# Two cross-attention layers in fp32: a third buffer for the small weights, the last value products planned to the end, and a first input load cut by contraction chunks

## The chip, the cores and the metric

The kernel runs on one core of a Trainium2 chip. The metric is the device time of one launch in microseconds. Before the change three runs took 2079.56, 2083.08 and 2083.56 us, median 2083.08. TensorE is called PE here, VectorE DVE, ScalarE ACT, GpSimd POOL and SyncE SP; SP issues most loads, POOL most stores.

## The reference, cut to what matters

There are 8 batches of 100 query rows with 640 channels, a context of 722 rows with 1024 channels (77 text rows, 645 image rows), and 20 heads of 32 channels. Layer 1 takes the output of layer 0. All is fp32.

```python
def layer(x, ctx, l):                       # heads split and merged as usual
    text, ip = ctx[:, :77], ctx[:, 77:]
    q = x @ Wq
    k, v = text @ Wk, text @ Wv             # text keys and values
    ki, vi = ip @ Wk_ip, ip @ Wv_ip         # image keys and values
    text_out = softmax(q k^T * scale) v
    if l == 0:
        ip_out = softmax(q ki^T * scale) vi
    else:                                   # layer 1
        pt = softmax(q @ k^T * scale)       # over all channels, not per head
        sem = (pt @ text) @ ip^T * scale    # one map for all heads
        ip_out = (softmax(q ki^T * scale + 0.5 * sem) * mask) vi
    return (text_out + ip_out) @ Wo + bo + x
```

## The kernel before, in words

**Projections.** Keys and values of the context are by far the largest matmuls. `seven` forms them with seven products of half-size blocks where the plain way has eight; it needs sums of weight quarters (`weight_sums`, L127) and of context quarters (`token_sums`, L212). `token_sums` puts two adds on DVE (`s1`, then `s2`) and two on POOL (`s3`, and `s4`, which reads `s2`).

**First stage (L222 to L407).** A pool named "first" holds what only this stage needs. SP loads x of batches 0 and 1 (tile `xt`, L227), five chunks of the query weights (`wq0`, 128 rows of the contraction each, L230), the rest of x in three loads, the text, then the K and V weights. PE forms the queries of layer 0 (`psq`, L253): for each pair g of batches, five contraction chunks k, and in each five output chunks c. Their results go out by POOL's queue. Then, in an order written out by hand (L388), text keys and values of both layers follow (`text_k`, whose first products are `pskt`, then the seven products `pskt_a` to `pskt_e`; `text_v`). The sums of the text (`s_text`) have a tile of their own, formed as soon as the text is there.

**Main stage.** A unit u is a layer and a batch (16 of them); a chunk c is four heads. The list `ORDER` has 80 steps of one unit and chunk each. In the last ten the two last units are interleaved: steps 70 to 79 are (14,0), (14,2), (15,0), (15,2), (14,1), (14,3), (15,1), (15,3), (14,4), (15,4). In step n PE does, by hand-written order: scores of the first 512 keys (`sc`, L837), transposes 0 and 1 of the previous step's probabilities (`pspt`, L922), transposes 2 and 3, scores of the other 210 keys, transposes 4 and 5, and the values (`pv`, L944) of the previous step. Copies of transposes to SBUF (`pt`) are done by DVE (L929), for j = 2 and 5 by ACT (L927). ACT does the exponentials (L861) and half of the scaling (L889), DVE the maxima (L853) and sums.

**The planner.** Between these pieces PE gets projection products for later units. `production` (L957) makes a list of tasks, each group with a stretch of steps (a, b), and `spread` gives each task a time inside it. `between(n, a, b, small)` issues all tasks whose time lies below n + b, and with `apart` takes one more from the next 0.4 of a step if otherwise two small pieces would stand side by side. The last products of the last two units are `fifth_chunk`: keys (`psk`, L669) with some values, planned for steps 72.9 to 76.9, then values alone (`psv`, L675) from 76.9 to 78.6. Each such block of 128 context rows has its x tile loaded (`x<-ip_t`) and its values stored in DRAM and loaded again as `v`.

**Small work.** For each pair g of units, five `out_piece` (L746, products `pso`, DVE add at L757) form the layer's output, and for layer 0 five `q_piece` (L766) form the queries of layer 1. Each piece reads one tile of weights of 320 KB, `wo` (o or q), loaded by `load_wo` (L739) on SP in a ring of two buffers; there are 55 such loads. The output of the last pair is made by `last_out` (L798, products `pso_last`, L804) from weights that stay in SBUF; its last call for a unit also adds the residual on DVE (L811) and issues the store on SP (L812). After step 79 follow `last_out(0)`, six transposes of the last step, values, `last_out(1)`.

The order of PE is fixed by hand in the main stage; that of DVE, ACT, POOL and SP is made by the framework's scheduler when the kernel is built. Buffers of a pool are rings: a load or a write into a ring's tile waits until the readers of the tile that lay there before are done.

Of the kernel before, what the change touches and what calls it, by code (L numbers as in the profile page):

```python
# [9 lines left out]
F32 = mybir.dt.float32  # L10
# [4 lines left out]
P = 128  # L15
B = 8
S = 100
# [10 lines left out]
NC_ = C // P  # L28
# [6 lines left out]
HK = NCC // 2  # L35
# [3 lines left out]
PAIRS = [(2 * i, 2 * i + 1) for i in range(NU // 2)]  # L39
# [5 lines left out]
def two_layer_xattn(  # L45
# [17 lines left out]
    nc = tc.nc  # L63
# [3 lines left out]
    wpool = ctx.enter_context(tc.tile_pool(name="w", bufs=1))  # L67
# [144 lines left out]
    def token_sums(a11, a12, a21, a22, s1, s2, s3, s4):  # L212
        nc.vector.tensor_tensor(s1, a21, a22, ALU.add)
        nc.vector.tensor_tensor(s2, s1, a11, ALU.subtract)
        nc.gpsimd.tensor_tensor(s3, a11, a21, ALU.subtract)
        nc.gpsimd.tensor_tensor(s4, a12, s2, ALU.subtract)
        return {1: a11, 2: a12, 3: s4, 4: a22, 5: s1, 6: s2, 7: s3}


    TH = B * NT // 2  # L220
    TR = TH - 2 * P
    with ExitStack() as es:  # L222
        fp = es.enter_context(tc.tile_pool(name="first", bufs=1))
        pj.append(es.enter_context(tc.tile_pool(name="ps_first", bufs=6, space=PSUM)))
        xt = fp.tile([P, B, NC_, S], F32, tag="x", name="xt")
        wq0 = []
        nc.sync.dma_start(xt[:, :2], x_t[:, :2])  # L227
        for k in range(NC_):
            t = fp.tile([P, C], F32, tag="wr", name=f"wq0_{k}", bufs=NCC)
            nc.sync.dma_start(t, wq[0][k * P : (k + 1) * P, :])  # L230
            wq0.append(t)
        for g in range(1, B // 2):
            nc.sync.dma_start(xt[:, 2 * g : 2 * g + 2], x_t[:, 2 * g : 2 * g + 2])
        text = fp.tile([P, NCC, B * NT], F32, tag="text", name="text")
# [12 lines left out]
        for g in range(B // 2):  # L247
# [16 lines left out]
                )  # L264
            nc.gpsimd.dma_start(q_d[0][g], t)

        st = fp.tile([P, 4, HK, TH], F32, tag="s", name="s_text")
        sums = token_sums(
            *(text[:, HK * h : HK * (h + 1), TH * i : TH * (i + 1)] for i in range(2) for h in range(2)),
            *(st[:, i] for i in range(4)),  # L270
        )

        def text_k(l):
            t = fp.tile([P, 2, 512], F32, tag="ev", name=f"kt4_{l}", bufs=2)
# [110 lines left out]
        def sums_of(kind):  # L385
            weight_sums(kind, {"v": HC, "k": 2 * P}[kind], (nc.vector, nc.gpsimd))

        with tc.manual_schedule(engines={mybir.EngineType.PE}):  # L388
            sums_of("k")
            text_k(0)  # L390
            load_wk(wkt[1])
            text_v(0)
            sums_of("v")
            load_left(0)
            text_v_blocks(0)
            load_wv(wvt[1])
            sums_of("k")
            text_k(1)
            load_wk(wki[0])
            left_v(0)  # L400
            load_left(1)
            left_text()
            text_v(1)
            sums_of("v")
            text_v_blocks(1)
            sums_of("k")
            left_v(1)  # L407
# [180 lines left out]
    LAST = PAIRS[-1]  # L588
# [150 lines left out]

    def load_wo(kind, src, g):  # L740
        for c in range(NC_):
            t = wpool.tile([P, NC_, P], F32, tag="wo", name=f"{kind}_{g}_{c}", bufs=2)
            nc.sync.dma_start(t, src.rearrange("(k p) n -> p k n", p=P)[:, :, c * P : (c + 1) * P])
            wos[kind, g, c] = t

# [52 lines left out]
    def last_out(i, ks_):  # L798
        g = len(PAIRS) - 1
        if ks_[0] == 0:  # L800
            last_ps[i] = product_ps(f"pso_last_{i}")
        for k in ks_:
            for c in range(NC_):
                nc.tensor.matmul(  # L804
                    last_ps[i][:, c * S : (c + 1) * S], lhsT=last_w[c][:, k, :], rhs=hsg[g][:, i, k, :],
                    start=(k == 0 and c == 0), stop=(k == NC_ - 1), skip_group_check=True,
                )
        if ks_[-1] < NC_ - 1:
            return
        r = resg[g][:, i].rearrange("p c s -> p (c s)")  # L810
        nc.vector.tensor_tensor(r, last_ps[i][:, : NC_ * S], r, ALU.add)  # L811
        nc.sync.dma_start(out[LAST[i] % B], resg[g][:, i])  # L812
# [99 lines left out]

    pts = {}

    def transposes(u, c, j):
        if j == 0:
            emit(len(later))
            pts[u, c] = one.tile([P, 6, 4 * S], F32, tag="pt", name=f"pt_{u}_{c}")
        rows = P if j < 5 else NTAIL
        ps = ps_pt.tile([P, 512], F32, tag="pt", name=f"pspt_{u}_{c}_{j}")  # L920
        for i in range(4):
            nc.tensor.transpose(  # L922
                ps[:rows, i * S : (i + 1) * S], pr[u, c][:, i, j * P : j * P + rows], ident[:S, :S]
            )
        dst, src = pts[u, c][:rows, j, :], ps[:rows, : 4 * S]
        if j % 3 == 2:
            nc.scalar.copy(dst, src)  # L927
        else:
            nc.vector.tensor_copy(dst, src)  # L929
# [27 lines left out]
    def production():  # L957

        plan = []
        for i in range(1, len(PAIRS) - 1):  # L960
            tasks = pair_tasks(PAIRS[i])
            at = max(n for n, (t, _) in enumerate(tasks) if t == 2.15) + 1
            if i == B // 2 - 1:

                tasks = tasks[:at] + [(0.0, lambda: second_weights("v"))] + tasks[at:]
                tasks.append((0.0, lambda: second_weights("k")))
            elif i == len(PAIRS) - 2:
                tasks = tasks[:at] + [(0.0, last_weights)] + tasks[at:]
            plan.append((10 * (i - 1) - AHEAD, 10 * i - AHEAD, tasks))
        n = 5 * LAST[0]  # L970
        every = list(range(NB))
        by_chunks = [blocks_of(every, lambda j, xs, r=r: two_chunks(r, j, xs)) for r in range(2)]
        fifth = [
            blocks_of(every, lambda j, xs: fifth_chunk("kv" if j < 2 else "k", j, xs)),
            blocks_of(every[2:], lambda j, xs: fifth_chunk("v", j, xs)),
        ]
        plan.append((n - 10 - AHEAD, n + 2.9, by_chunks[0] + by_chunks[1]))
        plan.append((n + 2.9, n + 6.9, fifth[0]))
        plan.append((n + 6.9, n + 8.6, fifth[1]))
        return [task for a, b, tasks in plan for task in spread(a, b, tasks)]  # L980

    def spread(a, b, tasks):
# [91 lines left out]
    with tc.manual_schedule(engines={mybir.EngineType.PE}):  # L1074
        for _, f in pair_tasks(PAIRS[0]):
            f()
        load_q(0)
        load_vt(0)
        load_k(0, 0)
        todo = production()  # L1080
        done = [0]

        def next_task():
            todo[done[0]][2]()
            if todo[done[0]][0] and later:
                emit(1)
            done[0] += 1

        def make(until):
            while done[0] < len(todo) and todo[done[0]][1] < until:  # L1090
                next_task()

        mark = [0]

        def apart(until):

            while done[0] < len(todo) and todo[done[0]][1] < until and not any(
                t for t, _, _ in todo[mark[0] : done[0]]
            ):
                next_task()  # L1100
            mark[0] = done[0]

        def between(n, a, b, small):

            mark[0] = done[0]
            for i, (_, f) in enumerate(small):
                make(n + a + (b - a) * (i + 1) / (len(small) + 1))
                apart(n + b + 0.4)
                f()
            make(n + b)  # L1110
            apart(n + b + 0.4)

        make(0.0)
        last = None
        for n, (u, c) in enumerate(ORDER):
            at = small_work(n)
            loads(n)
            scores(u, c, 0)
            if n == len(ORDER) - 1:
                load_v(*last)  # L1120
                load_v(u, c)
            between(n, 0.0, 0.4, at[0])
            if last:
                transposes(*last, 0)
                transposes(*last, 1)
            between(n, 0.4, 0.6, at[1])
            if last:
                transposes(*last, 2)
                transposes(*last, 3)
            scores(u, c, 1)  # L1130
            if n == NC_ * LAST[0] - 1:
                load_q(LAST[1])
            between(n, 0.6, 0.8, at[2])
            if n < len(ORDER) - 2:
                load_v(u, c)
            if n + 1 < len(ORDER):
                load_k(*ORDER[n + 1])
            if last:
                transposes(*last, 4)
                transposes(*last, 5)  # L1140
            between(n, 0.8, 1.0, at[3])
            if last:
                values(*last)
            last = (u, c)
        last_out(0, [NC_ - 1])
        for j in range(6):
            transposes(*last, j)
        values(*last)
        last_out(1, [NC_ - 1])


# [44 lines left out]
```

## Time and profile before

| what | value |
|---|---|
| runs, us | 2079.56, 2083.08, 2083.56 |
| profiled execution, us | 2088.13 |
| its span, us | 2086.4 |
| PE busy | 2058.5 us, 99% |
| DVE, ACT, POOL busy | 988.3, 862.8, 379.8 us |
| SP's hardware queue | 184.48 MB, 32.6% of 16 engines' span |
| first matmul | 5.63 us |
| end of the last `psq` | 41.44 us |
| steps 76, 77, 78 (start to start of scores) | 11.02, 12.42, 10.29 us |
| last matmul ends, span ends | 2082.5, 2086.4 us |

The profile is of one execution, and times in it run from the span's start. Busy times of engines overlap, so the table does not add up to the span. A wait is written as "engine, tile, line, what released it: us in total, times, longest us". In a timeline, a row is a run of equal instructions with its start, its length, and in brackets the idle time ahead of it on that engine and what ended it. The granted clock is what the throttle of PE allowed, 1.00 being full speed.

### The profile page before, as it was taken

How to read it: one execution, taken by the hardware profiler on the slowest of the kernel's cores; microseconds unless marked ns; L12 is line 12 of the kernel's file. 1: busy time of each engine (PE TensorE's matmuls, PEld its weight loads, DVE VectorE, ACT ScalarE, POOL GpSimd, SP SyncE). 2: the span in 40 equal slices, each digit the busy share in tenths (PEclk: the TensorE clock that was granted, in tenths of full speed). 3: DMA queues.
4: the chain of work that ended last, by engine and by line, in shares of the span. 5: the costliest groups of instructions: out<-in, count | busy, mean ns of one | idle time of the engine just before them, and what ended most of it. 6: DMA issues, size and time to landing. Idle time of an engine off the chain costs nothing. (4 is left out here: it accounts for less than half of the span.)

```text
span 2086.4 us, 41767 instructions
## 1 busy us (share of the span) xinstructions
PE 2058.5 (99%) x16690; PEld 1641.6 (79%) x16690; DVE 988.3 (47%) x2526; ACT 862.8 (41%) x2830; POOL 379.8 (18%) x409
## 2 busy tenths in 40 slices
PE   8999999999999999999999999999999999999998
PEld 8676787777777777787788877887888778889786
DVE  2111221345554554444464554445455455667565
ACT  1001000245434544344444544445444445566576
POOL 3213211111110111111141111111111113223120
PEclk9999999999999999999999999999999999999999
DMA  9345232323333443352544443353344344545482
GB/s 350 108 134 165 87 87 78 113 75 96 103 99 119 119 118 88 96 162 81 157 121 131 124 117 81 103 156 94 85 112 132 104 122 136 158 119 142 126 227 73
DMA packets 299104, 255.58 MB, mean 123 GB/s; under 512 B 43102, under 2 KB 267794, under 8 KB 298910
## 3 DMA queue, kind: packets, MB, share of 16 engines
q1 hardware_dynamic: 279374, 184.48, 32.6%
q0 software_dynamic: 19536, 68.43, 9.8%
q8 instruction: 132, 2.16, 0.4%
q14 instruction: 62, 0.51, 0.1%
HBM read 183.93 MB, written 68.93 MB: 121 GB/s over the span
## 5 line engine op out<-in xcount | busy, mean ns | idle before, releaser
L861 ACT ACTIVATE p<-sc,st 100x512 f32<-100x512 f32 (+1 forms) x320 | 166.5, 528 | 227.3 <-DVE st L846 227.3
L929 DVE COPY pt<-pspt 128x400 f32<-128x400 f32 x320 | 175.9, 569 | 122.4 <-PE pspt L922 119.4
L861 ACT ACTIVATE p<-p,st 100x512 f32<-100x512 f32 (+1 forms) x320 | 177.0, 555 | 134.9 <-DVE st L853 134.5
L889 ACT ACTIVATE p<-p,st 100x512 f32<-100x512 f32 x320 | 209.6, 714 | 48.6 <-DVE st L883 48.2
L922 PE MATMUL pspt<-ident,p 100*128 100x100 f32 (+1 forms) x1920 | 212.2, 251 | 7.2 <-DVE res L757 2.5
L922 PEld LDWEIGHTS pspt<-ident,p 100*128 100x128 f32 (+1 forms) x1920 | 187.8, 138 | 37.2 <-issue 5.5
L528 PE MATMUL psv_a<-wv,x 128*128 128x397 f32 (+1 forms) x560 | 185.3, 473 | 2.0 <-ACT vo L174 2.0
L927 ACT COPY pt<-pspt 128x400 f32<-128x400 f32 (+1 forms) x160 | 77.9, 487 | 254.8 <-PE pspt L922 254.7
L528 PE MATMUL psv_d<-wv,s 128*128 128x320 f32 (+1 forms) x560 | 174.7, 454 | 0.0
L552 POOL DMA_DIRECT2D v_d<-vo x70 | 39.5, 564 | 723.6 <-DVE gst L520 386.4
L846 DVE TENSOR_REDUCE st<-sc 100x2 f32<-100x1024 f32 (+1 forms) x120 | 126.2, 1052 | 68.2 <-ACT p L861 37.8
L528 PEld LDWEIGHTS psv_a<-wv,x 128*128 128x128 f32 x560 | 103.1, 189 | 65.9 <-issue 9.4
L853 DVE CUSTOM_DVE_ANT_0 p<-sc,sem 100x512 f32<-100x512 f32 (+1 forms) x320 | 139.6, 490 | 25.4 <-PE sc L837 25.3
L528 PEld LDWEIGHTS psv_d<-wv,s 128*128 128x128 f32 x560 | 103.6, 190 | 56.0 <-issue 6.6
L536 PEld LDWEIGHTS psk_a<-x,wk 128*128 128x128 f32 x1120 | 132.3, 191 | 12.7 <-issue 9.4
L837 PE MATMUL sc<-k,q 32*100 32x210 f32 (+1 forms) x1280 | 140.6, 509 | 1.2 <-ACT p L861 0.6
L564 POOL DMA_DIRECT2D k_d<-ko x70 | 58.2, 831 | 448.6 <-DVE ko L200 426.6
L536 PE MATMUL psk_d<-s,wk 128*128 128x128 f32 (+1 forms) x1120 | 139.7, 277 | 0.0
L536 PE MATMUL psk_a<-x,wk 128*128 128x128 f32 (+1 forms) x1120 | 139.1, 277 | 0.0
L536 PEld LDWEIGHTS psk_d<-s,wk 128*128 128x128 f32 x1120 | 131.2, 191 | 8.2 <-issue 3.3
L503 PE MATMUL psk<-x,wk 128*128 128x256 f32 (+1 forms) x560 | 131.6, 383 | 0.0
L503 PEld LDWEIGHTS psk<-x,wk 128*128 128x128 f32 x560 | 102.1, 189 | 23.2 <-issue 7.9
(207 smaller groups left out, 3403.5 us busy)
## 6 DMA issues: line engine op xcount, KB each, us to landing
x<-ip_t SPq DMA_DIRECT2D x84, 512.0 KB
k<-k_d SPq DMA_DIRECT2D x80, 322.5 KB
v<-v_d SPq DMA_DIRECT2D x80, 320.0 KB
v_d<-vo POOLq DMA_DIRECT2D x70, 320.0 KB, 2.6
k_d<-ko POOLq DMA_DIRECT2D x56, 320.0 KB, 6.8
x<-ip_t SPq DMA_DIRECT2D x22, 532.0 KB
o<-wo SPq DMA_DIRECT2D x35, 320.0 KB
q<-wq SPq DMA_DIRECT2D x20, 320.0 KB
```

The source lines that it names most:

```text
L503: nc.tensor.matmul(ps[:, : 2 * n], lhsT=W["k", 4][:, k, :], rhs=xs[j][:, :, k, :n], start=(k == 0), stop=(k == NCC - 1),)
L528: nc.tensor.matmul(ps[:, :m], lhsT=sums[which][:, k, :P], rhs=w[:, k, :], start=(k == 0 and not go_on), stop=(k == HK - 1), skip_group_che ...
L536: nc.tensor.matmul(ps[:, r * n : (r + 1) * n], lhsT=W["k", WHICH[which]][:, k, r * P : (r + 1) * P], rhs=sums[which][:, k, :], start=(r == ...
L564: nc.gpsimd.dma_start(k_d[u][:, :, n0 : n0 + n], ko[0][:, h, :, :n])
L837: nc.tensor.matmul(sc[:S, i, : k1 - k0], lhsT=qs_[u][rows, c, :], rhs=ks[u, c][rows, k0:k1], start=True, stop=True)
L846: nc.vector.tensor_reduce(st[:, part, heads[0] : heads[-1] + 1], sc[:S, heads[0] : heads[-1] + 1, :n], AX.X, ALU.max, negate=True,)
L853: nc.vector.tensor_tensor_reduce(out=p[:, i, k0 : k0 + n], in0=sc[:S, i, :n], in1=sems[u][:, k0 : k0 + n], scale=-1.0, scalar=3.0e38, op0= ...
L861: nc.scalar.activation(dst, dst if l else sc[:S, i, :n], AF.Exp, bias=st[:, part, i : i + 1], scale=-1.0 if l else 1.0, accum_out=st[:, 3 ...
L889: nc.scalar.activation(p[:, i, :KA], p[:, i, :KA], AF.Copy, scale=mul[:, 0, i : i + 1])
L922: nc.tensor.transpose(ps[:rows, i * S : (i + 1) * S], pr[u, c][:, i, j * P : j * P + rows], ident[:S, :S])
L927: nc.scalar.copy(dst, src)
L929: nc.vector.tensor_copy(dst, src)
```

## The change

- The first load of x is cut into five, one for each contraction chunk, each ahead of the weight chunk of the same k. One piece is 102 KB in rows of 400 bytes, where the load of before had 512 KB in rows of 4000 bytes.
- The tile of x gets the size of the text sums, 19,712 bytes per partition, and the two share one buffer. The text sums are formed by a function that is called behind the weight sums.
- The ring of `wo` has three buffers.
- The last value products are planned from step 76.9 to 78.95 instead of 76.9 to 78.6, and the reach ahead in `between` is 0.1 of a step instead of 0.4 from step 76 on.
- The add and store of the last output are a function of their own, called behind the last six transposes for the first of the two units. The first of these six copies goes to ACT.

```diff
-        xt = fp.tile([P, B, NC_, S], F32, tag="x", name="xt")
+        xt = fp.tile([P, 4 * HK * TH], F32, tag="x", name="xt")[:, : B * NC_ * S].rearrange(
+            "p (b k s) -> p b k s", b=B, k=NC_
+        )
         wq0 = []
-        nc.sync.dma_start(xt[:, :2], x_t[:, :2])
         for k in range(NC_):
+            nc.sync.dma_start(xt[:, :2, k], x_t[:, :2, k])
             t = fp.tile([P, C], F32, tag="wr", name=f"wq0_{k}", bufs=NCC)
             nc.sync.dma_start(t, wq[0][k * P : (k + 1) * P, :])
...
-        st = fp.tile([P, 4, HK, TH], F32, tag="s", name="s_text")
-        sums = token_sums(
...
+        sums = {}
+
+        def text_sums():
+            st = fp.tile([P, 4 * HK * TH], F32, tag="x", name="s_text").rearrange("p (i k n) -> p i k n", i=4, k=HK)
+            sums.update(
+                token_sums(
...
             sums_of("k")
+            text_sums()
             text_k(0)
...
-            t = wpool.tile([P, NC_, P], F32, tag="wo", name=f"{kind}_{g}_{c}", bufs=2)
+            t = wpool.tile([P, NC_, P], F32, tag="wo", name=f"{kind}_{g}_{c}", bufs=3)
...
-        if ks_[-1] < NC_ - 1:
-            return
+
+    def last_out_add(i):
+        g = len(PAIRS) - 1
         r = resg[g][:, i].rearrange("p c s -> p (c s)")
         nc.vector.tensor_tensor(r, last_ps[i][:, : NC_ * S], r, ALU.add)
         nc.sync.dma_start(out[LAST[i] % B], resg[g][:, i])
...
-        if j % 3 == 2:
+        if j % 3 == 2 or at_end and j == 0:
             nc.scalar.copy(dst, src)
...
-        plan.append((n + 6.9, n + 8.6, fifth[1]))
+        plan.append((n + 6.9, n + 8.95, fifth[1]))
...
+            near = 0.4 if n < NC_ * LAST[0] + 6 else 0.1
             for i, (_, f) in enumerate(small):
                 make(n + a + (b - a) * (i + 1) / (len(small) + 1))
-                apart(n + b + 0.4)
+                apart(n + b + near)
                 f()
             make(n + b)
-            apart(n + b + 0.4)
+            apart(n + b + near)
...
         for j in range(6):
-            transposes(*last, j)
+            transposes(*last, j, at_end=True)
+        last_out_add(0)
         values(*last)
         last_out(1, [NC_ - 1])
+        last_out_add(1)
```

More of the change, by code (lines that the diff above doesn't have):

```diff
@@ L265, in two_layer_xattn @@
             nc.gpsimd.dma_start(q_d[0][g], t)
-        st = fp.tile([P, 4, HK, TH], F32, tag="s", name="s_text")
-        sums = token_sums(
-            *(text[:, HK * h : HK * (h + 1), TH * i : TH * (i + 1)] for i in range(2) for h in range(2)),
-            *(st[:, i] for i in range(4)),
-        )
+        sums = {}
[3 more added lines that the diff above has]
+                token_sums(
+                    *(text[:, HK * h : HK * (h + 1), TH * i : TH * (i + 1)] for i in range(2) for h in range(2)),
+                    *(st[:, i] for i in range(4)),
+                )
+            )
         def text_k(l):
@@ L913, in two_layer_xattn, with transposes @@
     pts = {}
-    def transposes(u, c, j):
+    def transposes(u, c, j, at_end=False):
         if j == 0:
```

## The prediction

> **What bounds the kernel now.** I read the page's head first, then TensorE's waits, then the timeline around each long wait, then windows of 3.41 us around the places where the granted clock halves.
>
> ```profile
> span 2086.4 us, 41767 instructions
> PE 2058.5 (99%) x16690; PEld 1641.6 (79%) x16690; DVE 988.3 (47%) x2526; ACT 862.8 (41%) x2830; POOL 379.8 (18%) x409
> PE psq L253 <- DMA wq<-wq: 5.6, 1, 5.6
> PE pso L752 <- DMA o<-wo: 3.0, 2, 2.4
> ...
> PE pspt L922 <- DVE pt L929: 2.5, 2, 1.9
> ```
>
> Read: TensorE (PE) is busy 99% of the span, and no matmul is added or removed. Only its idle time (about 24 us, summed from the gaps of its timeline), its slow-clock time and the 3.9 us after its last matmul (2082.53 to 2086.4) can shrink. The three waits shown are what the change is near: the start, the small weights `o`, and copies of transposed probabilities. The last two lines hold two waits each; the timeline places them.
>
> ```profile
> 1790.30 2.76 PE L752 MATMUL pso<-hs,o 128*128 128x200 f32 x10 [2.42 <-DMA o<-wo]
> ...
> 2050.24 0.65 PE L922 MATMUL pspt<-ident,p 100*128 100x100 f32 x5 [0.18 <-ACT p L889]
> 2052.80 1.04 PE L922 MATMUL pspt<-ident,p 100*128 100x100 f32 x8 [1.90 <-DVE pt L929]
> 2053.77 0.80 PE L837 MATMUL sc<-k,q 32*100 32x210 f32 x8
> 2054.50 1.59 PE L922 MATMUL pspt<-ident,p 100*128 100x100 f32 x8
> 2056.67 1.90 PE L944 MATMUL pv<-pt,v 128*32 128x100 f32 x40 [0.58 <-ACT pt L927]
> ```
>
> Read: one wait for `o` is 2.42 us (the other is 0.56 at 1961.94); step 78 has idle times of 0.18, 1.90 and 0.58. After the 1.90 the same eight transposes take 1.59 instead of 1.04, and the values 1.90 instead of about 1.06: the clock has dropped. The windows (PE, PEld, DVE, ACT, POOL busy, then the granted clock, DMA share, GB/s) show it:
>
> ```profile
> 1787.84:1791.25 3.41, 0.99 (x7) 0.98 (x7) 0.57 (x1) 0.00 (x0) 1.08 (x2) 1.00 0.79 245
> 1791.25:1794.66 3.41, 3.41 (x18) 2.91 (x20) 0.54 (x2) 0.49 (x1) 0.72 (x1) 0.50 0.07 22
> 1944.85:1948.26 3.41, 2.36 (x23) 1.58 (x23) 2.76 (x14) 2.35 (x10) 0.00 (x0) 1.00 0.22 43
> 2050.66:2054.07 3.41, 1.51 (x19) 1.06 (x17) 2.75 (x9) 3.22 (x9) 0.00 (x0) 1.00 0.33 96
> 2054.07:2060.90 6.83, 6.25 (x73) 3.65 (x65) 4.38 (x20) 4.69 (x20) 0.00 (x0) 0.50 0.15 41
> ```
>
> Read: half clock follows a window in which PE was thinly busy, at 1791, 1948 (third line is the window before it) and 2054.
>
> **What the Trainium skill says.** "TensorE: Matmul & The Clock Gate", "What's actually happening": the clock halves after an idle window of about 3.4 us, and windows run free of the kernel's start. The trace agrees on the half and the 3.41 us unit, but the windows before were not idle (0.99, 2.36, 1.51 us busy), so I treat a thin window as a risk, not a certainty. Part 4 there says that transposes don't count as busy in the same way; the second and third windows are mostly transposes and fit. "DMA: Bandwidth & Descriptors", "Specifications": rows of 512 B or more are wanted for line rate; the first x load changes from 4000 B to 400 B rows, for which the trace has no row of its own. "SBUF — State Buffer", "SBUF: two separate sides": VectorE with two SBUF inputs and GpSimd exclude each other on a shared port; the trace agrees: a text sum took 2.79 us beside GpSimd's, 1.44 alone.
>
> **Start.** Before, the first matmul needs x of two batches (512 KB) and one weight chunk (328 KB), 840 KB; after, 102 + 328 = 430 KB. 410 KB less at the page's 350 GB/s of the first slice is 1.2 us. Bounds: the first 12 matmuls took 3.86 us, 322 ns each, against 168 ns later, so if full clock still arrives at 9.49 only half of it, 0.6, is won; 400 B rows at half rate make it 0.5; one transfer's fixed part less in the queue could make it 1.4. I take 1.2. Later chunks come each 1.23 us and feed 5 matmuls of 322 ns (1.6 us), so there's no new wait while slow; at full clock (0.84 us) the last chunk may be 0.2 late. SP issues five x pieces for one, 0.45 us each in its row: 1.8 us later for text and first K weights, needed on PE at 41 and on VectorE at 19; the data, not the issue, sets these.
>
> **Shared buffer.** Text sums now wait for the last `psq` matmul (41.44 before, so 40.2), where s1 ran at 19.02. On VectorE: s1 40.2 to 43.0 (2.79 beside GpSimd), the remaining weight sum 1.49 to 44.5, s2 1.44 to 45.9. Its reader `pskt_b` starts at 51.80 before, 50.6 now: slack 4.7, and beyond it each us costs one. GpSimd: s3 to 43.0 against a reader at 54.7; behind it the last q store and a weight sum (2.67), then s4 to about 50 against about 61. The K copies of ScalarE move with their products. Cost 0, hidden under 8 us of `pskt`.
>
> **Third buffer for `o` and `q`.** 55 loads of 320 KB use two buffers; with three, each stands one place earlier on SP, where it waits for the piece before. No load in SP's order stands behind a later release than before: the one moved ahead of a K load waits for piece 2, and that K load waits for scores at 1795.07 anyway. The load behind the 2.42 was issued at 1785.14 and used at 1790.30: 5 us; one piece earlier (1.7 us with its transposes and more) removes most or all of each wait, and three pieces arrive before the first. Gain 2.42 + 0.56 = 3.0, bounds 2.2 and 3.0. With the gap the thin window goes, and with it the half clock: ten `pso` matmuls took 2.76 against about 1.71, eight transposes 1.65 against 1.04, so 1.6.
>
> **Tail plan.** Steps 76, 77, 78 last 11.02, 12.42, 10.29: 33.73, with 3, 4 and 0 half-products. In TensorE's order after: 2 (`psk` second half, `psv2` first), 3, 2 (`psv4` both). Without products a step has 5.10 us of its own: step 76 less 1.90 + 1.81 + 1.88 of products and 0.33 idle. So 3 x 5.10 + 7 x 1.87 = 28.4. ScalarE's busy time per step is about 10, which three steps can't undercut much, so I add 2.3 of waits (bounds 0.8 and 3.5): 30.7, gain 3.0. The slow scores after 2058.83 (2.04 against 1.12) go too: 0.9. Sum 3.9; of it 2.9 is clock (0.8 + 1.0 + 0.2 + 0.9), 1.0 idle. What is late next: `psv3` and `psv4` finish later, and their v store and load have some 10 us before values need them. The x blocks for the last products are loaded in buffers that the previous products free; below.
>
> **End.** The first of the last six copies goes to ScalarE: `pspt` at 2077.01 waited 0.62 for VectorE, which did an output add (0.68) first. The moved output add still stands ahead of the copies in VectorE's order, so its move does nothing; the ScalarE copy frees T2 at about 2076.5. Then each later step follows: 0.6 (0 to 0.8).
>
> **Sum** against the profiled execution (2088.13, 1.7 around its span): 1.2 + 3.0 + 1.6 + 3.9 + 0.6 = 10.3, so 2077.8. The runs' median is 2083.08, 5 less: presumably some clock drops are missing there already, so I count idle terms whole (1.2 + 3.0 + 1.0 + 0.6 = 5.8) and clock terms (1.6 + 2.9) by half, 2.2: 8.0, so 2075.
>
> **Rivals.** A: all gains show, 2075 (own range 2072 to 2078.5). B: ScalarE sets the tail (10 us per step, 3.2 busy of 3.4 in the fourth window) or thin windows recur elsewhere, since a transposes-only stretch remains in every step; the tail's 3.9 falls to 0 or below and a clock drop stays: 2083.1 less about 3 = 2078 to 2082. C: the drop at 1948 goes as well (about 3.3: `sc`, `pv` and `psm` at twice their time): 2069 to 2072. D: the change doesn't do what it says, as the waits are set by DMA rate and not by buffers (0.79 DMA share in the first window): start gain alone or less, 2082 to 2084. E, slower: x loads of the last products are late. After, the interval from the end of `psv2`'s second half to the start of `psv4` is about 8.8 us; the load takes 0.2 to issue behind the release, 1.0 of queue, and 6.2 (issued about 2015, landed by 2022): 7.4, slack 1.4. From 7.6 us of latency on it decides; at 10 us, three loads late by 2 to 3 us each, with a clock drop of 1.7 behind each, about 12, which turns the 8 into a loss of 4 or more: above 2087.3. Against it: x loads of that size near there show only 0.5 of PE wait (two times).
>
> **Numbers.** A 55%, B 25%, C 10%, D 5%, E 5%. The measurement tells 0.2% (4.2 us: 2078.9 and 2087.2). Faster: A 53 of 55, B 13, C 10, D 2: 0.78; same: the rest of A 2, of B 12 and of D 3: 0.17; slower: E, 0.05. The range 2070 to 2081 leaves out D, E, the top quarter of B and the bottom third of C.
>
> **What would show it.** First matmul at about 4.4. No wait of `pso` for `o`, and full clock at 1791. Text sums on VectorE at about 40 with no new PE wait before `pskt_b`. Steps 76 to 78 of about 10.2 each, with no half clock there; if they hold waits for ScalarE's `p` or `pt`, B is right; PE waits of `psv` for x loads mean E. Last transposes with waits under 0.3. The prediction is wrong if the clock drops move rather than vanish, or the median before is not 5 below its profile for the reason I gave.

## The result and the profile after

| | before | after |
|---|---|---|
| median of 6 runs, us | 2083.44 | 2076.19 |
| lowest and highest, us | 2079.56, 2084.58 | 2073.27, 2076.96 |
| span of the profiled execution, us | 2086.4 | 2075.2 |
| mean granted clock of the profiled execution | 0.996 | 0.999 |

The ratio is 0.9965, 95% interval 0.9952 to 0.9978: 7.3 us faster (4.6 to 10.0). A second measurement on another occasion (e12_after below) gave 0.9965 again, 0.9952 to 0.9977. The forecast was 2075.0, some 8 us under before.

The page of the changed kernel, its head, and TensorE's waits:

```profile
span 2075.2 us, 41767 instructions
PE 2051.8 (99%) x16690; PEld 1639.7 (79%) x16690; DVE 988.0 (48%) x2525; ACT 861.9 (42%) x2831; POOL 381.7 (18%) x409
```

```profile
PE psq L255 <- DMA wq<-wq: 4.9, 1, 4.9
...
PE sc L846 <- ACT p L884: 1.9, 4, 0.9
...
PE pv L953 <- ACT pt L936: 0.9, 1, 0.9
```

The waits of `pso` for `o` and of `pspt` for VectorE's 1.9 are gone from the list; waits for ScalarE stand in the tail's place. Busy time of PE fell by 6.7 us with the same 16690 matmul instructions: that is slow clock that is gone, for no instruction was taken away.

TensorE's order is the same up to step 76, so the n-th matmul of one trace can be set against the n-th of the other. This gives the account of the 11.2 us between the two profiled spans (start in the trace after, less start in the trace before):

| up to | difference, us | what happened since the line above |
|---|---|---|
| first matmul | -0.75 | less data to wait for |
| matmul instruction 17 of `psq` | +0.15 | full clock at 10.57 instead of 9.49 |
| 1000 to 13000 instructions | +0.3, then 0.0 | 0.35 less of a wait near 1067 |
| scores at 1791 (1794.79 before) | -3.8 | wait for `o` 2.4, half clock about 1.3 |
| 1948.4 (1954.64) | -6.2 | half clock at 1948 absent |
| `pso` at 1954.88 (1961.94) | -7.1 | second wait for `o`, and the rest of that half clock |
| start of step 76 | -7.6 | x loads and others, 0.5 |
| start of step 79 | -10.0 | steps 76 to 78: 31.33 instead of 33.73 |
| first `pso_last` of step 79 | -10.9 | scores at full clock |
| last matmul | -11.4 | the last copies |
| end of the span | -11.2 | 0.2 more after it |

The timeline of PE in the changed kernel, at the loads of `o`, in step 78 and at the end:

```profile
1783.22 3.55 PE L760 MATMUL pso<-hs,o 128*128 128x200 f32 x20
...
1787.78 1.96 PE L760 MATMUL pso<-hs,o 128*128 128x200 f32 x10
...
2046.72 1.07 PE L953 MATMUL pv<-pt,v 128*32 128x100 f32 x40 [0.89 <-ACT pt L936]
2047.60 0.36 PE L953 MATMUL pv<-pt,vt 82*32 82x100 f32 x8
2048.82 1.12 PE L846 MATMUL sc<-k,q 32*100 32x512 f32 x8 [0.86 <-ACT p L884]
...
2065.66 0.99 PE L931 MATMUL pspt<-ident,p 100*128 100x100 f32 x8 [0.24 <-ACT pt L936]
```

The ten `pso` matmuls start without a wait and take 1.96 us for 2.76. In step 78 the wait of 1.90 for a PSUM buffer is gone, 0.89 and 0.86 for ScalarE have come. The last copies wait 0.24 for 0.62. The window that holds the first of the two new waits (columns as before: PE, PEld, DVE, ACT, POOL, clock, DMA share, GB/s):

```profile
2044.91:2048.33 3.42, 2.16 (x60) 1.71 (x56) 2.62 (x16) 2.93 (x16) 0.77 (x2) 1.00 0.25 75
```

PE is still busy for only 2.16 of 3.42, but no half clock follows. VectorE around the text sums, whose buffer is now shared, GpSimd's text sum beside them, and the matmul that reads `s2`, from the timeline of the changed kernel:

```profile
40.22 1.49 DVE L132 TENSOR_TENSOR wvt<-wv,wv 128x1280 f32<-128x1280 f32 x1 [8.77 <-DMA wv<-wvt]
41.79 1.44 DVE L213 TENSOR_TENSOR s_text<-text 128x1232 f32<-128x1232 f32 x1
41.83 4.04 POOL L215 TENSOR_TENSOR s_text<-text 128x1232 f32<-128x1232 f32 x1 [4.87 <-PE psq L255]
43.15 4.08 DVE L133 TENSOR_TENSOR wvt<-wvt,wv 128x1280 f32<-128x1280 f32 x1
47.15 1.43 DVE L214 TENSOR_TENSOR s_text<-s_text,text 128x1232 f32<-128x1232 f32 x1
...
51.95 2.24 PE L296 MATMUL pskt_b<-s_text,wkt 128*128 128x308 f32 x8
```

VectorE's sums start behind the last `psq` matmul and end at 48.6, 3.4 us before their reader. PE waits for none of them.

### The profile page after: what moved, and what is told of

Same layout as the page of the kernel before. It is cut to its first block, busy times and chain, and to the rows that moved or that the text cites. A ratio compares the mean times of both kernels' runs of the same rounds, so it can differ in the third digit from the quotient of the medians.

```text
span 2075.2 us, 41767 instructions
## 1 busy us (share of the span) xinstructions
PE 2051.8 (99%) x16690; PEld 1639.7 (79%) x16690; DVE 988.0 (48%) x2525; ACT 861.9 (42%) x2831; POOL 381.7 (18%) x409
## 3 DMA queue, kind: packets, MB, share of 16 engines
q8 instruction: 132, 2.16, 0.4%
```

## The experiments

Each was measured beside runs of the kernel before on the same chip: for the first group 52 runs of before (median 2085.2), for the second 25 (2083.55), for the third 19 (2084.91). The mean granted clock of before was 0.9968, 0.9970 and 0.9970 in them. A step of 0.001 in the mean clock is 2085 x 0.001 = 2.1 us of full-speed time. The slow clock at the start is not in this mean: that of the first profile comes out of its later half clocks alone. Ratios are to before, with the 95% interval in brackets.

### The four parts alone

**Ring and shared buffer (e1_ring).** The kernel before, with

```diff
-            t = wpool.tile([P, NC_, P], F32, tag="wo", name=f"{kind}_{g}_{c}", bufs=2)
+            t = wpool.tile([P, NC_, P], F32, tag="wo", name=f"{kind}_{g}_{c}", bufs=3)
```

and the shared tile with `text_sums()` behind `sums_of("k")`.

> Before with only the third buffer of wo; the text sums share the buffer of x as in the change (with a buffer of their own the pool first would need 103.06 KB per partition where 102.94 are left), the load of x stays whole. Theory (the two waits of pso for o are a matter of buffers, 2.42 and 0.56 us): both waits below 0.1, the window before 1791 busy and at full clock; 3.0 us of idle time gone and 1.3 to 1.6 of slow clock; the text sums late without a PE wait. Time 3 to 5 us under before. Rival (the DMA rate sets the wait): a wait for o of over 1 us stays at that place, time within 1.5 us of before. Rival (the sums are late): PE waits before pskt_b or pskt_c, each us of it lost.

Measured: 0.9975 (0.9969 to 0.9982), 5.2 us faster; mean clock 0.9976. No wait of `pso` for `o` is left, no PE wait before the text sums' readers. So the wait is one of buffers, though the DMA engines are busy around it (a share of 0.92 in the window from 1787.61). In its profile the half clocks of 1791 and 1948 are absent, that of the tail is there. The two windows are the one before it and the one with it:

```profile
2041.73:2045.14 3.41, 1.93 (x16) 0.77 (x12) 2.63 (x10) 3.14 (x8) 0.93 (x2) 1.00 0.18 55
2045.14:2055.38 10.24, 9.05 (x84) 6.10 (x85) 6.31 (x27) 7.11 (x27) 0.00 (x0) 0.50 0.21 60
```

The half clock lasts 10.24 us here, three windows, for 6.83 in the first profile. It lasts 10.24 in e2_split and e4_end too, so it is the first profile that is short.

**First load of x (e2_split).** The kernel before, with

```diff
-        nc.sync.dma_start(xt[:, :2], x_t[:, :2])
         for k in range(NC_):
+            nc.sync.dma_start(xt[:, :2, k], x_t[:, :2, k])
```

> Before with only the first x load cut by contraction chunks; the text sums keep their own buffer. In the changed kernel the first matmul came 0.75 us earlier (4.88) but full clock 1.08 later (10.57), so the last psq ended 0.15 later. Theory (the clock's windows of 3.41 us run free of the kernel's start, so the slow time after the first matmul is drawn anew in each execution, 3.4 to 6.8 us): first matmul at 4.9, first full clock 3.4 to 6.9 later, psq ends 36.0 plus or minus 1 us after the first matmul; time 0.7 under before on the mean, lost in the spread of the runs. Rival (rows of 400 bytes slow the loads so that PE waits or warms up later): gaps between psq matmuls above 0.1 us, or full clock again near 10.6.

Measured: 0.9999 (0.9990 to 1.0007): no gain that the runs can tell. First matmul 4.49, full clock 8.81 (4.32 later), last `psq` ends at 40.68, 36.19 after the first matmul. No gap over 0.1 us among the `psq` matmuls.

**Tail plan (e3_tail).** The kernel before, with

```diff
-        plan.append((n + 6.9, n + 8.6, fifth[1]))
+        plan.append((n + 6.9, n + 8.95, fifth[1]))
...
+            near = 0.4 if n < NC_ * LAST[0] + 6 else 0.1
...
-                apart(n + b + 0.4)
+                apart(n + b + near)
...
-            apart(n + b + 0.4)
+            apart(n + b + near)
```

> Before with only the planner's edits (8.95 and the reach of 0.1 from step 76). Theory: steps 76 to 78 sum to 31.3 us (33.73 before), no half clock at 2054, slow scores gone: 3.3 us between the last x wait and the first pso_last, time 2 to 3.5 under before. The waits that are left in step 78 are for ScalarE (pt and p, 0.9 each). Rival (it is only the clock drop that was won): the idle time in the three steps is as before, about 3 us, and runs without a drop are as fast before as after: time within 1 us.

Measured: 0.9981 (0.9974 to 0.9988), 4.0 us faster; mean clock 0.9986. Its PE waits:

```profile
PE sc L837 <- ACT p L875: 1.9, 4, 0.9
...
PE pso L752 <- DMA o<-wo: 1.8, 2, 1.3
...
PE pv L944 <- ACT pt L927: 0.9, 1, 0.9
```

The waits for ScalarE are those of the changed kernel, so they belong to this part. The wait for `o` is there, as the ring is that of before, but its longest is 1.3 us this time, and the half clock at 1791 is absent. The rival is half right: the gaps of steps 76 to 78 sum to 2.99 us in the kernel before and still to 2.51 in the changed one, so idle time hardly moved, and nearly all that is won is clock (0.9986 for 0.9968 is 3.7 us). It was wrong in its time, within 1 us of before, which took runs without the drop to be common. The profiles say otherwise: half clock in steps 76 to 79 is there in all four with the old tail and no filling (before, e1_ring, e2_split, e4_end), and in one of the eight with the new tail (e11_best). That at 1791 is there in four of the six with two buffers of `wo` and in none of the eight with three.

**End (e4_end).** The kernel before, with

```diff
-        if j % 3 == 2:
+        if j % 3 == 2 or at_end and j == 0:
             nc.scalar.copy(dst, src)
...
-            transposes(*last, j)
+            transposes(*last, j, at_end=True)
```

> Before with only the first of the last six copies on ScalarE; the output add stays where it is. Theory: the wait of pspt for VectorE's copy at the end (0.62) falls to about 0.24 for ScalarE's copy, the last matmul ends 0.4 us earlier after its pv, time 0.2 to 0.6 under before, not to be told apart by the runs. Rival (the move of the output add behind the copies is what won it): the wait stays at 0.6.

Measured: 0.9995 (0.9986 to 1.0003), nothing the runs can tell. In the profile the wait of 0.62 for VectorE's copy is gone and one of 0.24 for ScalarE's has come, with the output add where it was. So the copy, not the move of the add, is what does it.

The four ratios sum to 5.2 + 0.2 + 4.0 + 1.0 = 10.4 us. The half-widths of their intervals (1.4, 1.8, 1.5, 1.8) make about 3.3 together. The changed kernel was measured once more, as e12_after.

> The changed kernel as it is, once more beside the others. Alone, ring and shared buffer gave -5.2 us, the load -0.2, the tail -4.0, the end -1.0 by their ratios: 10.4 in sum. Theory (they add, and the first measurement of -7.3 plus or minus 2.7 was on its low side): 8 to 10.5 us under before. Rival (they overlap, since each takes part of the same clock drops): 6 to 8 under.

Measured: 2077.22 median, 0.9965 (0.9952 to 0.9977), 7.3 us faster, on the side of overlap; but 10.4 with 3.3 either way and 7.3 with 2.6 either way do not exclude each other, so this stays open. The clock shows no sign of overlap: the rises of the four parts (0.0008, -0.0005, 0.0018, 0.0005) sum to 0.0026, and together they give 0.0022 here and about 0.0026 in the first measurement.

### Is it the thin window, and what fills one?

**Matmuls as filling (e5_fill).** The kernel before, with work that nobody reads in the wait of step 78:

```diff
                 transposes(*last, 1)
+                if n == len(ORDER) - 2:
+                    ps = product_ps("fill")
+                    for _ in range(12):
+                        nc.tensor.matmul(ps[:, :P], lhsT=ident, rhs=ident, start=True, stop=True)
```

> Before, with twelve matmuls of 128x128 by 128 (about 1.3 us, read by nobody) added behind transposes 0 and 1 of step 78, where TensorE waits 1.90 us for a PSUM buffer. The work of the kernel is whole, the planner is that of before. Theory (the thin window makes the clock drop of 2047 to 2061, and the drop costs 2 to 3 us beyond the wait): the step keeps its length up to the wait's end, as the filling lies in idle time, no half clock follows it, steps 78 and 79 are 2 to 3 us shorter together, time 1 to 3 under before. Rival (the drop comes from something else, such as the transposes themselves): half clock is there as before, time the same or up to 1.5 longer.

Measured: 0.9991 (0.9985 to 0.9998), 1.9 us faster with more work than before; mean clock 0.9989 for 0.9970. From its timeline, and the windows behind the filling:

```profile
2044.55 2.87 PE L1129 MATMUL fill<-ident 128*128 128x128 f32 x24
2047.25 0.85 PE L922 MATMUL pspt<-ident,p 100*128 100x100 f32 x8
...
2050.37 1.07 PE L944 MATMUL pv<-pt,v 128*32 128x100 f32 x40 [0.89 <-ACT pt L927]
...
2052.47 1.73 PE L837 MATMUL sc<-k,q 32*100 32x512 f32 x8 [0.86 <-ACT p L875]
```

```profile
2049.44:2052.85 3.41, 1.66 (x53) 1.28 (x56) 2.20 (x14) 2.98 (x18) 0.00 (x0) 1.00 0.06 19
2052.85:2056.26 3.41, 3.41 (x18) 2.13 (x11) 3.09 (x10) 3.25 (x7) 0.00 (x0) 0.50 0.29 82
```

Where the filling is, the clock stays full; the next window, with waits of 0.89 and 0.86, is thin in its turn, and in this execution it drops. These are the same two waits as in the changed kernel, in which the window fell otherwise and held. Twelve fp32 matmuls are 24 instructions and took 2.87 us, not the 1.3 I had counted; the transposes behind them still came at full clock, and the step was not longer (10.12 us, 10.29 before). The 2 to 3 us expected from steps 78 and 79 did not all come: from step 76 to the first `pso_last` of step 79 this profile takes 35.2, the first one of before 35.7, the three with the longer half clock 36.5. The filling is also about 1 us longer than the wait that it fills, so the time falls by less than the clock alone would give (3.8).

**Transposes as filling (e10_fillt).** The same, with `range(26)` and

```diff
-                        nc.tensor.matmul(ps[:, :P], lhsT=ident, rhs=ident, start=True, stop=True)
+                        nc.tensor.transpose(ps[:, :P], ident, ident)
```

> Before, with 26 transposes of 128x128 (about 2.8 us, read by nobody) in the place in step 78 where e5_fill had matmuls of the same length. In e5_fill no half clock followed at 2046 to 2057, one of 3.4 us at 2053 took its place in the profile, and the mean clock of its runs rose from 0.997 to 0.999. Theory (the throttle counts transposes less than matmuls, as the windows of 2.4 us busy with transposes dropped too): half clock follows as in the kernel before, mean clock 0.997, time as before or up to 0.5 longer. Rival (busy is busy): as in e5_fill, mean clock 0.999, time 1.5 to 2 under before.

Measured: 0.9994 (0.9985 to 1.0002); mean clock 0.9988, as with matmuls. My theory falls, and the rival holds for the clock. The time is 1.3 us under before, not distinguishable from nothing, though the clock alone would give 3.7; about 1 us of that is again the filling's own length, and the rest is not accounted for. From its timeline, and its windows:

```profile
2047.53 3.00 PE L1129 MATMUL fill<-ident 128*128 128x128 f32 x26
```

```profile
2046.34:2049.76 3.42, 3.24 (x33) 3.01 (x30) 3.24 (x10) 3.15 (x9) 0.17 (x1) 1.00 0.39 117
2049.76:2053.17 3.41, 2.84 (x32) 2.23 (x29) 2.17 (x11) 1.92 (x8) 0.00 (x0) 1.00 0.06 17
2053.17:2056.58 3.41, 2.23 (x56) 1.28 (x56) 2.19 (x11) 2.81 (x15) 0.00 (x0) 1.00 0.16 46
```

So a window that is filled with transposes keeps the full clock. The statement of the Trainium skill ("TensorE: Matmul & The Clock Gate", "Part 4: PE-mode transpose") that transposes don't count as busy in the same way, with which I had read the thin windows, is not borne out for these fp32 transposes (mean clock 0.9988 with them, 0.9989 with matmuls); the measurement decides.

### Who sets the tail now?

The changed kernel, with the copy of transpose 5 on VectorE in steps 76 to 79 (e6_copies):

```diff
-        if j % 3 == 2 or at_end and j == 0:
+        if (j == 2 or j == 5 and (u, c) not in ORDER[-5:-1]) or at_end and j in (0, 5):
```

> The changed kernel, with the copy of transpose 5 on VectorE instead of ScalarE in steps 76 to 79. Theory (ScalarE sets the length of the tail's steps now): the wait of pv for ScalarE's pt in step 78 (0.89) goes, that of sc for ScalarE's p (0.86) shrinks, 0.8 to 1.7 us less than the changed kernel's 2076.2 and its tail. Rival (VectorE is as full there): a wait for VectorE of the same size takes its place, time within 0.5 of the changed kernel.

Measured: 2077.07 median, 0.9963 (0.9951 to 0.9976), that of the changed kernel. Its PE waits:

```profile
PE sc L846 <- ACT p L884: 2.5, 4, 1.1
PE pv L953 <- DVE pt L938: 1.8, 4, 0.7
```

The wait of `pv` is now 0.73 for VectorE where it was 0.89 for ScalarE, and that of the scores has grown to 1.15. Steps 76 to 78 sum to 32.0 us for 31.3. The rival holds: both engines are full there, and one copy moved is no gain.

### The start

**Rows of 800 bytes (e7_rows).** The changed kernel, with x given once more in the order partition, pair, chunk, batch:

```diff
-            nc.sync.dma_start(xt[:, :2, k], x_t[:, :2, k])
+            nc.sync.dma_start(xt[:, 0, k], x_p[:, 0, k])
```

> The changed kernel, with x given once more in an order in which the first pieces have rows of 800 bytes instead of 400. Theory (rows of 400 bytes load more slowly, so the first matmul came only 0.76 us earlier on the mean of three profiles, 4.68 against 5.44, where 410 KB less at 350 GB/s would be 1.2): first matmul at 4.2 to 4.4, and more than 4.40 MB moved in the first 15 us. Rival (the start of the transfers sets it, the rate not yet being 350 GB/s in the first microseconds): first matmul at 4.5 to 4.9.

Measured: first matmul 4.42, 4.57 MB in the first 15 us, time 0.9960 (0.9946 to 0.9975). With rows of 400 bytes and this issue order the profiles give 4.49 to 4.88, and 4.40 to 4.53 MB. But by 5 us it had moved 0.81 MB, and those with rows of 400 bytes 0.80 to 0.82. One profile, at the theory's edge: the rows cost 0.2 us or nothing. Undecided.

**Pieces of x on ScalarE's queue (e8_actq).** `nc.scalar.dma_start` for the five pieces, else the changed kernel.

> The changed kernel, with the five first x pieces issued by ScalarE's queue instead of SP's, so that the first x piece and the first weight chunk are issued side by side. Theory (the first matmul waits for the second issue, 0.5 us behind the first, and for the data): first matmul at about 4.3 instead of 4.5 to 4.9. Rival (the data's rate sets it, and pieces on two queues share it): first matmul within 0.2 of 4.7. In either case the time is that of the changed kernel within 1 us.

Measured: first matmul 3.97 (4.3 expected), last `psq` ends at 39.67; time 2074.71 median, 0.9953 (0.9939 to 0.9966). By 5 us 1.01 MB had moved. The theory holds for the first matmul: pieces issued one behind the other on SP reach it later. It is one profile, but e11_best below, with the same queue, has 4.03.

**Work in the idle start (e9_warm).** The changed kernel, with

```diff
         wq0 = []
+        wz = fp.tile([P, 2 * S], F32, tag="wz", name="wz")
+        nc.vector.memset(wz, 0.0)
+        wps = product_ps("warm")
+        for _ in range(11):
+            nc.tensor.matmul(wps[:, : 2 * S], lhsT=wz[:, :P], rhs=wz, start=True, stop=True)
```

> The changed kernel, with eleven matmuls of a zeroed tile (128x128 by 200, 322 ns each at half clock, 3.5 us, read by nobody) ahead of the first q matmul, in TensorE's idle start. Theory (full clock comes a drawn 3.4 to 6.8 us after TensorE's first work, so work in the idle start brings it forward by some 3.5 us): full clock at 5 to 8.5 us after the span's start, where the five profiles so far have 8.8 to 10.8; psq ends 1.3 to 2 us sooner after its first matmul; 1 to 2 us less than the changed kernel. Rival (the clock warms by real work only, or by time from the start): full clock at 8.5 to 11 as before, no gain.

Measured: full clock at 4.92; time 2075.24 median, 0.9956 (0.9943 to 0.9970). Its timeline:

```profile
1.17 5.82 PE L233 MATMUL warm<-wz 128*128 128x200 f32 x22 [1.17 <-DVE wz L230]
6.83 34.00 PE L260 MATMUL psq<-xt,wq 128*128 128x200 f32 x200
```

Eleven fp32 matmuls are 22 instructions and reach to 6.8, past the landing of the data, but all 200 of `psq` then run at full clock: 34.0 us for 36.87 in the changed kernel, and they end at 40.82 for 41.75. Work on zeros that nobody reads starts the clock too, so the rival falls (one profile). At 163.65, however, TensorE stands 0.92 us with no releaser in the profile, which it doesn't in the changed kernel, and the 0.93 is lost. What that is stays open.

**Both (e11_best)**, with four matmuls ahead.

> The changed kernel, with the first x pieces issued by ScalarE's queue and four matmuls of a zeroed tile ahead of the first q matmul (2.7 us, read by nobody; eleven took 5.8 us and delayed the first q matmul to 6.83, though psq then ended at 40.82 for 41.75). Theory (both gains of the start add): first q matmul at 4.0, full clock at 4.2 to 7, psq ends at 38.5 to 39.3, some 2 to 3 us under the changed kernel. Rival (what is won at the start is lost by 200 us, as text or weights come late): psq ends as said, but the last pskt or the work to 200 us is not earlier by the same amount.

Measured: first q matmul 4.03, last `psq` at 39.76 (38.5 to 39.3 expected), time 2077.88 median, 0.9966 (0.9953 to 0.9978). Full clock came at 7.38, 6.21 after TensorE's first work and no earlier than in the kernel with ScalarE's queue alone (7.26), and the standstill of 0.66 is there at 164.22. Its profile has a half clock of one window at 2048.55. The two gains of the start did not add, and no version here is shown to beat the changed kernel: the intervals of the best two (0.9939 to 0.9966 and 0.9943 to 0.9970) cover its 0.9965.

## Why the prediction was right

Its sign, its size (8 us, measured 7.3) and its rank of parts (ring and tail large, start and end small) held. By its steps:

- **Start: the term was too large.** "I take 1.2" became 0.75 at the first matmul in this profile, and 0.9 on the mean (six profiles with the whole load: 5.28 to 6.11, mean 5.55; four with the cut load on SP: 4.49 to 4.88, mean 4.64). The bytes were not the error: ahead of the first matmul 0.65 to 0.78 MB have moved, for 1.12 to 1.35 with the whole load. The error was to take one rate for both. By 5 us the four profiles with the cut load on SP have moved 0.80 to 0.82 MB, the six with the whole load 0.91 to 1.03, and the two with the pieces on ScalarE's queue 1.01 and 1.03. SP issues its transfers one in every 0.5 us there, and a piece of x brings only 102 KB; with rows of 800 bytes on SP it is 0.81 MB too. So the one queue, more than the rows of 400 bytes, goes with the slower start. The end of `psq`, which counts, moved by +0.15 here (41.60 to 41.75; the 41.44 of the table ahead is the start of what follows) and by -0.7 on the means (41.84 to 41.12). The bound "only half of it" named the reason: full clock came 2.98 to 5.89 us after the first matmul in the twelve profiles without added work at the start, and this draw is larger than the gain. My expectation of 3.4 to 6.8 for it was too high at both ends. One reading was off without harm: a chunk feeds five fp32 matmuls, which are ten instructions of 322 ns, so later chunks had twice the slack that I gave them.
- **Shared buffer: cost 0, right.** The order of the port was not as said: the first text sum took 1.44 and not 2.79, and the weight sum behind it 4.08 instead of 1.49. The end at 45.9 became 48.6, the slack 4.7 became 3.4. The Trainium skill's exclusion of VectorE with two SBUF inputs and GpSimd ("SBUF — State Buffer", "SBUF: two separate sides") fits these rows: VectorE's sum ran at its full speed first, GpSimd's beside it took 4.04 instead of 2.81, and VectorE's next instruction ended 1.4 us after GpSimd's, which is about its own length.
- **Ring: right.** Both waits are gone, in the changed kernel and in e1_ring. One size was off: with two buffers the longer wait is 1.28 to 2.48 in six profiles, mean 2.04, and the shorter, 0.49 to 0.60, is there in only three of them, so that 3.0 was on the high side.
- **Tail: right in kind, 3.3 of 3.9 against the first profile.** The steps went to 31.33 (30.7 forecast): 2.51 of idle, where I had put 2.3, and 0.4 more of work than the 28.4. Idle time so fell by 0.5 and not by 1.0; the rest, 2.8, is the clock, as said (2.9). Against the three profiles in which the half clock lasts 10.24, the same stretch falls from 36.5 to 32.4, by 4.1, and e3_tail alone measured 4.0. The x loads caused no wait over 0.2.
- **End: 0.43 for 0.6,** by ScalarE's copy, and 0.2 of it is given back after the last matmul.
- **Clock terms by half: the step that failed.** It rested on "presumably some clock drops are missing there already". Some are, but far from half. Over 96 runs the kernel before has a mean clock of 0.9969, 0.0031 below full. Its profile has half clock for 17.07 us and for the last 1.6 us of its span, together 0.0045 of the span lost. A typical run so keeps about 70% of that loss, and is 2.9 us shorter than the profile by its clock. The changed kernel has 0.9992 to 0.9995: a rise of about 0.0024, which is 5.0 us, where I counted 2.2. With the idle terms as measured (start 0.7, ring 2.04 and on the mean 0.3, tail 0.5, end 0.4: 3.9, where I counted 5.8) this makes 8.9, above the measured 7.3 but inside its interval. The idle terms were too large and the clock term too small; that the two errors nearly cancel is luck.
- **Rivals.** B came true in part: ScalarE does set the tail, but its price is in the 31.33. C's event, the drop at 1948 gone, happened in this profile (2.5 us), but it comes and goes: of the six profiles with two buffers of `wo` only the first and e4_end have it, and none of the eight with three. D and E found nothing.

## What to carry to other kernels

At 99% busy the gain still lies in few places: list TensorE's gaps one by one, and look at the granted clock in the window behind each, since the slow matmuls behind a gap can cost more than the gap (in the tail 2.8 us of the 3.3 won were clock). Spread work that is still to be done into thin steps: the tail's gain of 4 us came with only 0.5 us less idle, and even useless matmuls in the gap paid. Before counting a gain at the kernel's start, compare it with what is drawn there in each execution, and take the clock from many runs, not from the profile alone.

## What the runs showed that was not expected

**Which windows bring half clock.** Half clock followed windows in which PE was busy for 0.84 to 1.93 us in the last three hundred us of six profiles (the very end left aside), and also 2.36 and 2.49 at about 1944, mostly of transposes and values; it did not follow 2.13 to 2.47 in others there, nor 1.74 at 2042 in e8_actq, nor 1.45 to 2.02 at 1064, where the matmuls are 128x128 by 320. Busy time alone doesn't decide, and what does stays open.

**A coin of 2 us.** In nine of the fourteen profiles (both kernels among them) `psv_a` waits 1.6 to 2.0 us near 1067, in five it doesn't, and the work behind is then 2.2 us earlier. VectorE and GpSimd in the kernel before:

```profile
1060.20 4.26 DVE L897 TENSOR_TENSOR p<-p,st 100x532 f32<-100x532 f32 x1
...
1060.16 1.43 POOL L216 TENSOR_TENSOR s<-x,s 128x512 f32<-128x512 f32 x1
1061.40 2.48 POOL L132 TENSOR_TENSOR wkt<-wk,wk 128x1024 f32<-128x1024 f32 x1
```

and in e4_end, which doesn't differ there:

```profile
1060.13 1.97 DVE L897 TENSOR_TENSOR p<-p,st 100x532 f32<-100x532 f32 x1
...
1063.50 2.35 POOL L132 TENSOR_TENSOR wkt<-wk,wk 128x1024 f32<-128x1024 f32 x1 [1.98 <-DMA wk<-wki]
```

If the weights have landed when GpSimd ends its sum, it starts the next one and VectorE's product waits for both, 4.26 us; if they are late, VectorE gets in between, 1.97. The fourteen profiles divide by this without exception: 4.26 to 4.28 us and no wait of GpSimd for the weights in the nine, 1.80 to 1.97 and a wait of 0.68 to 1.98 in the five. The chain goes by VectorE's maxima to ScalarE's copy of `vo` to TensorE. Weights that landed earlier thus went with about 2 us lost.
